# Cross-attention on one core: where the first block of x is loaded and split, and when the probability chunks are taken

## The chip, the cores and the metric

The kernel runs on one core of one Trainium2 chip. The metric is the device time of a run in microseconds; the figure given for a kernel is the median over its runs. One further execution is profiled, and every duration of a single instruction in this document comes from such a profile.

## The reference, cut to what matters

The input x (`hidden_states`) has 32 blocks of 512 rows and 640 columns, the context (`encoder_hidden_states`) 32 blocks of 77 rows and 1024 columns. For each block, text cross-attention with 20 heads of 32 is computed:

```python
q = _heads(hidden_states @ to_q_w)
h_txt = _sdpa(q, _heads(ehs_txt @ to_k_w), _heads(ehs_txt @ to_v_w))
# _sdpa: softmax(q k^T / sqrt(32)) v, for each head
out = _merge(h_txt) + ...
out = out @ to_out_w + to_out_b
out = (out + residual) / RESCALE          # RESCALE = 1, residual = x
```

The context has 77 rows in each block, so the parts for objects, others and images are empty and are left out of the kernel.

## The kernel before, in words

All products are made in a split form: an operand is written as a high part and the remainder (`split`: ScalarE copies to a rounded type, VectorE or GpSimd subtracts), and each product is three matmuls (high x high, high x low, low x high: `PAIRS`).

The program has two stages. The first makes keys and values of all 32 x 77 = 2464 context rows, in five groups of at most 512 rows (`GROUPS_KV`, the last has 416). For a group, `context` loads and transposes context rows and splits them into eight tiles `ct`; `keys` multiplies them with `wk_s` (five column tiles j, each a chain of 24 matmuls into PSUM `pk`), splits the result (`ks`) and stores it to DRAM (`k_dram`); `context_values` makes the values of 128 rows and half of the columns (a "half": 24 matmuls into `pv`), splits them into `vs`, and after the second half stores them to `v_dram`. In the last group there are four row tiles (three of 128, one of 32), so eight halves. Stage one is placed by a scheduler, which follows the program's order as far as operands allow.

The second stage is written out by hand (`manual_schedule`): each engine does its instructions in the program's order, and so does the queue of SyncE (SP), which issues all DMAs. Its unit is a slot n = 5 b + j: block b of 512 rows, and one of five column tiles j with 4 heads each; there are 160 slots. `slot(n)` (L557) issues, in this order mixed over the engines:

- scores of slot n in four row tiles t (`scores`, L368), each with a maximum on VectorE (`nm`) and four exponentials on ScalarE (`exps`, L386);
- queries of slot n + 1 (`queries`, L333, 15 matmuls in parts of 6 and 9), then `split_q` (L344 to L350), which fills `qt` with three forms of q;
- for slot n - 1: reciprocal of the sums, `normalize` on GpSimd (L401), `transpose_p` on VectorE (L408) into `z`, and four stores of z to a DRAM tile `pd`; this is a "chunk" of probabilities, which comes back in another layout by `load_p` into `raw`;
- for an older slot, its chunk is "taken": `cast_p`, `rest_p`, `last_p` split `raw` into `pp` on ScalarE, VectorE and GpSimd (L432 to L446), `values` (L460) multiplies it with the block's values `vb`, and `split_a` splits the result into `at`;
- for the block before or the one before that, two pieces of the output projection (`piece`, L490, 12 matmuls each), addition of bias and residual, and the store;
- refills of keys and values of the next block, loads of the next x (`load_x`), its transposes in place (`transpose_x`) and splits (`split_x`, five column tiles `xt`).

Which slot takes which chunk is in `takes` and `seconds`. The distance is `LAG` = 3 slots. But the tiles for `raw`, `pp`, `at` and the output weights `wo_s` (pool `late`) lie where the weights `wv_s` and the tiles `ct` of stage one lay, and their PSUM banks where `pv` was; they exist only after the last halves of values are made. The first `LATE` slots therefore run without takes, and some chunks are taken late:

```python
    LATE = 4
    LAG = 3
    takes = {n + LAG: n for n in range(N) if n + LAG > LATE}
    seconds = {LATE + n: n for n in range(LATE + 1 - LAG)}
    takes[LATE + 1], seconds[LATE + 1] = 1, 2
```

So in slot 4 chunk 0 is taken as a `second`, at the very end of the slot; in slot 5 chunk 1 in the slot's usual place and chunk 2 as a `second`; from slot 6 on there is one take a slot, of chunk n - 3. The projection begins in slot 7 (`PIECES`: block 0 is projected in slots 7 to 11).

Between the two stages stands a run-up: x of block 0 is loaded after the last keys are stored, two halves of values are made while it is under way, x is transposed (L273) and split (L280, L281), four more halves follow, then the first queries; the last two halves stand in slots 1 and 3 (`beside`). The tiles of x (`xs`, one buffer; `xt`, seven) lie in the pool `main`, which takes the room of the pool `kvt` (raw weights, raw context, `wk_s`, `ks`).

Of the kernel before, what the change touches and what calls it, by code (L numbers as in the profile page):

```python
# [8 lines left out]
F32 = mybir.dt.float32  # L9
FPR = mybir.dt.float32r  # L10
# [40 lines left out]
def kernel(  # L51
# [52 lines left out]
        nc.scalar.copy(hi, src)  # L104
        nc.vector.tensor_tensor(lo, src, hi.bitcast(F32), ALU.subtract)

    def split_weights(pool, dst, w, k, permuted=True, scale=None):


        raw = pool.tile([P, C], F32, tag="wraw", name="wraw", bufs=3)  # L110
        if permuted:
            rows = w.rearrange("(q c i) n -> c q i n", q=4, i=Q)[k]
            for q in range(4):
                nc.sync.dma_start(raw[q * Q : (q + 1) * Q, :], rows[q])  # L114
        else:
            nc.sync.dma_start(raw, w[k * P : (k + 1) * P, :])
        if scale is not None:
            scaled = pool.tile([P, C], F32, tag="wscaled", name="wscaled", bufs=1)
# [6 lines left out]
    wq_s = const.tile([P, NC_, 2, C], FPR, name="wq_s")  # L125


    kvp = tc.alloc_tile_pool(name="kvp", bufs=1, side="right")
    kvt = tc.alloc_tile_pool(name="kvt", bufs=2, side="right")
    psk = tc.alloc_tile_pool(name="psk", bufs=8, space=PSUM)  # L130
    wv_s = kvp.tile([P, NK, 2, C], FPR, name="wv_s")
    wk_s = kvt.tile([P, NK, 2, C], FPR, name="wk_s", bufs=1)
# [3 lines left out]
    def context(g0, gn):  # L136
        na = gn // Q
        src = ehs_flat[g0 : g0 + gn, :].rearrange("(a j) (q u) -> q j a u", j=Q, q=4)
        cts.clear()
        loads = {}  # L140
        k0 = 0
        for kn in (1, 1, 2, 4) if g0 == 0 else (4, 4):
            loads[k0] = kn
            k0 += kn
        for k in range(NK):
            if g0 == 0:
                split_weights(kvt, wk_s[:, k], wk, k)
            if k in loads:
                kn, k0 = loads[k], k
                cs = kvt.tile([P, G // Q, 4 * Q], F32, tag="cs", name="cs", bufs=3)  # L150
                for q in range(4):
                    nc.sync.dma_start(
                        cs[q * Q : (q + 1) * Q, :na, : kn * Q], src[q, :, :, k * Q : (k + kn) * Q]
                    )
            raw = kvt.tile([P, G], F32, tag="craw", name="craw")
            nc.vector.transpose(
                raw[:, :gn].rearrange("p (a j) -> p a j", j=Q),
                cs[:, :na, (k - k0) * Q : (k - k0 + 1) * Q],
            )
            ct = kvp.tile([P, 2, G], FPR, tag="ct", name="ct", bufs=9)  # L160
            split(ct[:, 0, :gn], ct[:, 1, :gn], raw[:, :gn])
            cts.append(ct)
# [20 lines left out]
                        ks[w * 64 : w * 64 + 64, int(half != w), :gn].bitcast(F32),  # L183
                    )

    values_of = {}

    def context_values(g0, gn, t0, h, pool):

# [20 lines left out]
        if h == 1:  # L210
# [2 lines left out]
                vs[:tn].rearrange("p h d a -> p (h d a)").bitcast(F32),  # L213
            )


    zero = kvt.tile([P, G], FPR, name="zero", tag="craw")
    nc.vector.memset(zero.bitcast(F32), 0.0)
# [6 lines left out]
        nc.tensor.matmul(warm, zero[:, :P], zero, start=True, stop=True)  # L225
    for g0, gn in GROUPS_KV:
        context(g0, gn)
        if g0 == 0:
            for k in range(NK):
                for j in range(NC_):  # L230
                    keys(g0, gn, j, k)
            for k in range(NK):
                split_weights(kvt, wv_s[:, k], wv, k)
            nc.sync.dma_start(bias, bo.unsqueeze(0).to_broadcast([P, C]))
        else:
            for j in range(NC_):
                for k in range(NK):
                    keys(g0, gn, j, k)
        if g0 == GROUPS_KV[1][0]:
            for k in range(NC_):  # L240
                split_weights(kvt, wq_s[:, k], wq, k, scale=SCALE)
        if g0 == GROUPS_KV[2][0]:
            for k in range(NC_):
                ws = kvt.tile([P, 2, C], FPR, tag="ws", name="ws", bufs=1)
                split_weights(kvt, ws, wo, k, permuted=False)
# [11 lines left out]
    psv = tc.alloc_tile_pool(name="psv", bufs=3, space=PSUM, side="right", reuse_waits="tile")  # L257
    late = []

    xts, raws, pps, ats, xss, pds, sms, pqs, pas, xrs, pos = ({} for _ in range(11))  # L260

    def load_x(b, quarters=range(4)):

        if b not in xss:
            xss[b] = main.tile([P, S // Q, C // 4], F32, tag="xs", name="xs")
        xs = xss[b]
        src = x[b].rearrange("(a j) (q u) -> q j a u", j=Q, q=4)
        for q in quarters:
            nc.sync.dma_start(xs[q * Q : (q + 1) * Q, :, :], src[q])

    def transpose_x(b, i):
        part = xss[b][:, 4 * i : 4 * i + 4, :].rearrange("p a u -> p (a u)")
        nc.vector.transpose(part, part)  # L273

    def split_x(b, c, engine=nc.gpsimd):

        xt = main.tile([P, 2, S], FPR, tag="xt", name="xt", bufs=7)
        src = xss[b].rearrange("p (a t) u -> p t a u", t=NQ)[:, :, :, c * Q : (c + 1) * Q]
        parts = [xt[:, i, :].rearrange("p (t a j) -> p t a j", t=NQ, j=Q) for i in range(2)]
        nc.scalar.copy(parts[0], src)  # L280
        engine.tensor_tensor(parts[1], src, parts[0].bitcast(F32), ALU.subtract)  # L281
        xts[b, c] = xt

    kbs, vbs, pnb = [], [], []
    for g, (j0, nj) in enumerate(GROUPS):
# [140 lines left out]
    def cast_p(n):  # L428

        raw = raws[n]  # L430
        pp = late[0].tile([P, 5, S], FPR, tag="pp", name="pp", bufs=1)
        nc.scalar.copy(pp[:, 0:2, :], raw[:, 0:2, :])  # L432
        pps[n] = pp
# [33 lines left out]

    def split_a(n):
        if n >= N - NC_ + 1:
            at = main.tile([P, 2, S], FPR, tag="xt", name="at", bufs=7)  # L470
        else:
            at = late[0].tile([P, 2, S], FPR, tag="at", name="at", bufs=8)
        split(at[:, 0, :], at[:, 1, :], pas.pop(n))
        ats[n] = at
# [46 lines left out]
            if h == 1:  # L521
                nc.sync.dma_start(out[b, t * P : (t + 1) * P, :], xr)

    LATE = 4
    LAG = 3

    takes = {n + LAG: n for n in range(N) if n + LAG > LATE}
    seconds = {LATE + n: n for n in range(LATE + 1 - LAG)}
    takes[LATE + 1], seconds[LATE + 1] = 1, 2

# [9 lines left out]
    def take(m):  # L540
        values(m)
        split_a(m)
# [11 lines left out]
        elif j == 3:  # L554
            load_values(b, 1, segments)

    def slot(n, beside=None):  # L557
        b, j = divmod(n, NC_)
        ahead, more = n + 1 < N, b + 1 < B
        back, first = PIECES[j]  # L560
        bo_, has_out = b - back, b >= back
        xsplits = SPLIT_X.get(j, ((), ())) if more else ((), ())
        turns = TRANSPOSE_X.get(j, ((), (), ())) if more else ((), (), ())
        taken, second = takes.get(n), seconds.get(n)

        refill(b, j, 0)
        if taken is not None:
# [204 lines left out]
```

## Time and profile before

| | before |
|---|---|
| time, median of 3 runs | 2010.02 us (2009.55 to 2010.04) |
| profiled execution, its own time | 1996.0 us |
| its span, first to last instruction | 1994.2 us |
| mean granted TensorE clock | 0.991 |
| busy: PE, weight loads, VectorE, ScalarE, GpSimd | 98%, 88%, 68%, 80%, 49% |
| DMA | 423.54 MB, 212 GB/s over the span |

In the profile's lines PE is TensorE's matmuls, PEld its weight loads, DVE VectorE, ACT ScalarE, POOL GpSimd, SP SyncE's queue. Times are microseconds from the span's start. `L386` is line 386 of the kernel. "out<-in" names the tiles written and read, "x40" is a count, and "[6.43 <-ACT pp L432]" says that the engine stood idle for 6.43 us before the instruction, and that the last thing it waited for was ScalarE writing `pp` in line 432. A line of windows gives the stretch, its length, the busy time of each engine with the number of instructions, the clock that TensorE was granted (1.00 is full), the share in which the 16 DMA engines were busy, and GB/s.

### The profile page before, as it was taken

The page shows a single profiled execution, that of the slowest core. Times are in us where ns is not written, and L with a number is a line of the kernel's source. Part 1 is how long each engine was busy: PE and PEld are TensorE (multiplying, and loading weights), DVE is VectorE, ACT ScalarE, POOL GpSimd, SP SyncE. Part 2 cuts the span into 40 slices and gives each one's busy share as a digit, 9 for nine tenths or more (in the row PEclk, how much of TensorE's full clock was granted, in tenths as well). Part 3 has the DMA queues.
Part 4 walks back from the last instruction along what each step waited for, and adds up shares of the span by engine and source line. Part 5 has one row for each costly group of instructions (what it writes and reads, how often), then busy time and mean ns, then how long its engine had stood idle before and what let it go on. Part 6 is the DMA issues. An engine that isn't in the chain of part 4 may idle for free.

```text
span 1994.2 us, 38184 instructions
## 1 busy us (share of the span) xinstructions
PE 1950.5 (98%) x11012; PEld 1760.0 (88%) x11012; DVE 1352.5 (68%) x2159; ACT 1598.2 (80%) x6377; POOL 982.8 (49%) x617
## 2 busy tenths in 40 slices
PE   8999997899999999999999999999999999999998
PEld 7889986788899999899899898999989898988997
DVE  4443225777777777777777777777777777777774
ACT  3321128899999999999899999999999899998993
POOL 0000023555555555655556655566655566555554
PEclk9999998999999999999999999999999999999999
DMA  7994366889988889898988899998888888888975
GB/s 172 225 261 107 106 148 146 232 213 232 226 225 226 229 221 231 216 229 212 232 225 224 220 225 230 229 233 222 219 223 223 223 223 225 224 218 230 228 198 164
DMA packets 555997, 423.54 MB, mean 212 GB/s; under 512 B 170192, under 2 KB 459502, under 8 KB 555790
## 3 DMA queue, kind: packets, MB, share of 16 engines
q1 hardware_dynamic: 555789, 421.10, 83.9%
q8 instruction: 91, 1.49, 0.3%
q14 instruction: 117, 0.95, 0.2%
HBM read 245.61 MB, written 175.32 MB: 211 GB/s over the span
## 4 chain that ended last, share of the span: by engine, by line
PE 78%; DMA 9%; SPq 4%; POOL 3%; ACT 2%; issue 2%; DVE 2%; DVEq 0%; ACTq 0%; POOLq 0%
PE po L490 24%; PE pq L333 24%; PE pa L460 13%; PE sc L368 9%; PE pv L197 4%; PE pk L168 4%; DMA raw<-pd 3%; POOL pn L401 2%; DMA pd<-z 2%; SPq L114 1%; DMA xs<-in_x_dram 1%; POOL pp L446 1%; ACT pn L386 1%; DMA k_dram<-ks 1%; DMA cs<-in_ctx_dram 1%
## 5 line engine op out<-in xcount | busy, mean ns | idle before, releaser
L386 ACT ACTIVATE pn<-sc,nm 128x77 f32<-128x77 f32 x2560 | 802.0, 330 | 44.6 <-DVE nm L376 33.8
L401 POOL TENSOR_TENSOR pn<-pn,rs 128x1232 f32<-128x1232 f32 x160 | 364.4, 2277 | 670.3 <-DVE rs L396 643.9
L490 PE MATMUL po<-wo_s,at 128*128 128x320 f32 x3840 | 626.9, 312 | 2.2 <-DVE xr L518 2.2
L333 PE MATMUL pq<-xt,wq_s 128*128 128x512 f32 x2400 | 622.4, 400 | 0.0
L490 PEld LDWEIGHTS po<-wo_s,at 128*128 128x128 f32 x3840 | 566.3, 189 | 2.7 <-DVE xr L518 2.5
L386 ACT ACTIVATION_READ_ACCUMULATOR pn<-sc,nm 128x1 f32 x2560 | 533.1, 208 | 0.0
L333 PEld LDWEIGHTS pq<-xt,wq_s 128*128 128x128 f32 x2400 | 429.6, 190 | 77.4 <-POOL xt L281 0.2
L376 DVE TENSOR_REDUCE nm<-sc 128x4 f32<-128x308 f32 x640 | 294.6, 460 | 298.2 <-PE sc L368 291.0
L460 PE MATMUL pa<-pp,vb 128*128 128x512 f32 x1280 | 334.9, 402 | 18.4 <-ACT pp L432 9.8
L460 PEld LDWEIGHTS pa<-pp,vb 128*128 128x128 f32 x1280 | 243.5, 198 | 62.8 <-POOL pp L446 14.3
L408 DVE STREAM_TRANSPOSE z<-pn 128x1280 f32<-128x1280 f32 x160 | 241.5, 1509 | 36.2 <-POOL pn L401 31.6
L439 DVE TENSOR_TENSOR pp<-raw,pp 128x1024 fp32r<-128x1024 f32 x160 | 196.1, 1226 | 82.4 <-ACT pp L432 72.2
L368 PEld LDWEIGHTS sc<-kc,qt 128*128 128x128 f32 x1280 | 212.8, 189 | 27.2 <-ACT qt L348 4.2
L446 POOL TENSOR_TENSOR pp<-raw,pp 64x512 fp32r<-64x512 f32 x160 | 209.4, 1309 | 37.0 <-ACT pp L438 19.8
L368 PE MATMUL sc<-kc,qt 128*128 128x154 f32 x1280 | 222.9, 255 | 4.5 <-DVE qt L350 3.9
L350 DVE TENSOR_TENSOR qt<-pq,qt 64x512 fp32r<-64x512 f32 x320 | 214.3, 670 | 7.5 <-ACT qt L344 3.1
L281 POOL TENSOR_TENSOR xt<-xs,xt 128x512 fp32r<-128x512 f32 x157 | 200.0, 1296 | 19.4 <-ACT xt L280 12.5
L483 POOL TENSOR_TENSOR xr<-xr,bias 128x640 f32<-128x640 f32 x128 | 201.3, 1573 | 9.7
L348 ACT CAST qt<-qt 64x512 fp32r<-64x512 f32 x320 | 198.8, 621 | 8.9
L368 PE MATMUL sc<-kb,qt 128*128 128x308 f32 x640 | 196.1, 306 | 1.2 <-ACT qt L344 1.2
L432 ACT CAST pp<-raw 128x1024 fp32r<-128x1024 f32 x160 | 170.1, 1063 | 29.7 <-DMA raw<-pd 28.9
L104 ACT CAST at<-pa 128x512 fp32r<-128x512 f32 x160 | 94.9, 593 | 82.2 <-PE pa L460 81.1
(41 smaller groups left out, 1530.8 us busy)
## 6 DMA issues: line engine op xcount, KB each, us to landing
pd<-z SPq DMA_DIRECT2D x640, 160.0 KB, 3.6
raw<-pd SPq DMA_DIRECT2D x160, 512.0 KB, 4.3
xs<-in_x_dram SPq DMA_DIRECT2D x128, 320.0 KB, 7.0
xr<-in_x_dram SPq DMA_DIRECT2D x128, 320.0 KB, 3.8
out_dram<-xr SPq DMA_DIRECT2D x128, 320.0 KB, 3.2
raw<-pd SPq DMA_DIRECT2D x160, 128.0 KB, 4.4
v_dram<-vs SPq DMA_DIRECT2D x19, 640.0 KB, 4.0
k_dram<-ks SPq DMA_DIRECT2D x80, 128.0 KB, 2.4
```

What stands on the lines that cost most here:

```text
L281: engine.tensor_tensor(parts[1], src, parts[0].bitcast(F32), ALU.subtract)
L333: nc.tensor.matmul(pqs[n], wq_s[:, k, a, j * P : (j + 1) * P], xts[b, k][:, c, :], start=(k == 0 and m == 0), stop=(k == NC_ - 1 and m == 2),)
L350: nc.vector.tensor_tensor(qt[r, 1 + w, :], pq[r], qt[r, 0, :].bitcast(F32), ALU.subtract)
L368: nc.tensor.matmul(sc[:, cols], qt[:, m, t * P : (t + 1) * P], keys_, start=(m == 0), stop=(m == 2),)
L376: nc.vector.tensor_reduce(nm, sc[:, :KCOLS].rearrange("p (h k) -> p h k", k=NKEY), AX.X, ALU.max, negate=True)
L386: nc.scalar.activation(pnb[n % 2][:, at, :NKEY], sc[:, i * NKEY : (i + 1) * NKEY], AF.Exp, bias=nm[:, i : i + 1], accum_out=sms[n][:, at : ...
L401: nc.gpsimd.tensor_tensor(pf, pf, rs.unsqueeze(2).to_broadcast([P, NQ * HPC, NKEY]), ALU.mult)
L408: nc.vector.transpose(z.rearrange("p b t j -> p t b j"), pn.rearrange("p (t h) k -> p t (h k)", t=NQ).rearrange("p t (b i) -> p t b i", i=Q),)
L446: nc.gpsimd.tensor_tensor(pp[64:, 4, :], raw[:64, 2, :], pp[:64, 4, :].bitcast(F32), ALU.subtract)
L460: nc.tensor.matmul(pas[n], vb[:, t, :, a], pp[:, c, :], start=(m == 0), stop=(m == len(PASSES) - 1),)
L483: nc.gpsimd.tensor_tensor(xrs[b, t], xrs[b, t], bias, ALU.add)
L490: nc.tensor.matmul(pos[b, t, h][:, :HALF], ats[b * NC_ + j][:, a, t * P : (t + 1) * P], wos[0][:, j, c, h * HALF : (h + 1) * HALF], start= ...
```

## The change

1. Raw weights and raw context get pools of their own (`kvw`, `kvc`), which are released when the last group's context is in `ct`. A new pool `xpool` with `xs` and `xt` takes that room, so that x of block 0 is loaded, transposed and split inside stage one, beside the last group's keys; x of block 1 is loaded right after.
2. In the run-up the queries of block 0 come first, then four halves of values with the transposes of block 1's x and two of its splits between them. The other four halves stand in slots 0 and 1, two in each.
3. `LATE` is 2, and all chunks are taken three slots after their own (`takes` alone; `seconds` is gone). The output weights' loads, which stand in slots `LATE` to `LATE + 2`, come two slots earlier with it.

Subtractions of block 0's x are all on GpSimd (before, three of five on VectorE). The number of matmuls does not change.

```diff
-    def split_weights(pool, dst, w, k, permuted=True, scale=None):
-        raw = pool.tile([P, C], F32, tag="wraw", name="wraw", bufs=3)
+    def split_weights(dst, w, k, permuted=True, scale=None):
+        raw = kvw.tile([P, C], F32, tag="wraw", name="wraw", bufs=3)
...
+    kvw = tc.alloc_tile_pool(name="kvw", bufs=1)
     kvp = tc.alloc_tile_pool(name="kvp", bufs=1, side="right")
     kvt = tc.alloc_tile_pool(name="kvt", bufs=2, side="right")
+    kvc = tc.alloc_tile_pool(name="kvc", bufs=3, side="right")
...
-                cs = kvt.tile([P, G // Q, 4 * Q], F32, tag="cs", name="cs", bufs=3)
+                cs = kvc.tile([P, G // Q, 4 * Q], F32, tag="cs", name="cs", bufs=3)
...
     for g0, gn in GROUPS_KV:
         context(g0, gn)
+        if g0 == GROUPS_KV[-1][0]:
+            kvw.release()
+            kvc.release()
+            xpool.append(
+                ctx.enter_context(tc.tile_pool(name="xpool", bufs=1, reuse_waits="tile"))
+            )
+            load_x(0)
+            for i in range(NQ):
+                transpose_x(0, i)
+            for c in range(NC_):
+                split_x(0, c)
+            load_x(1)
...
-    LATE = 4
+    LATE = 2
     LAG = 3
 
-    takes = {n + LAG: n for n in range(N) if n + LAG > LATE}
-    seconds = {LATE + n: n for n in range(LATE + 1 - LAG)}
-    takes[LATE + 1], seconds[LATE + 1] = 1, 2
+    takes = {n + LAG: n for n in range(N)}
...
-    def slot(n, beside=None):
+    def slot(n, beside=()):
...
-        xsplits = SPLIT_X.get(j, ((), ())) if more else ((), ())
-        turns = TRANSPOSE_X.get(j, ((), (), ())) if more else ((), (), ())
-        taken, second = takes.get(n), seconds.get(n)
+        xsplits = SPLIT_X.get(j, ((), ())) if more and n > LATE else ((), ())
+        turns = TRANSPOSE_X.get(j, ((), (), ())) if more and b else ((), (), ())
+        taken = takes.get(n)
...
-        if beside:
-            beside()
+        if len(beside) > 0:
+            context_values(*beside[0], psv)
         s = scores(n, 3)
...
         exps(n, 3, *s)
+        if len(beside) > 1:
+            context_values(*beside[1], psv)
         if has_out:
             piece(bo_, first + 1)
...
-        if second is not None:
-            cast_p(second)
-            rest_p(second)
-            last_p(second)
-            take(second)
-            if second + 2 in pds and second + 2 not in takes.values():
-                load_p(second + 2)
...
     with tc.manual_schedule(engines=ENGINES):
         g0, gn = GROUPS_KV[-1]
-        load_x(0)
         load_keys(0, 0)
-        for h in range(2):
-            context_values(g0, gn, 0, h, psv)
-        for i in range(NQ):
-            transpose_x(0, i)
-        for c in range(NC_):
-            split_x(0, c, nc.gpsimd if c % 2 else nc.vector)
-        load_x(1)
-        for t0 in (P, 2 * P):
-            for h in range(2):
-                context_values(g0, gn, t0, h, psv)
+        halves = [(g0, gn, t0, h) for t0 in range(0, gn, P) for h in range(2)]
         queries(0, 0, NC_)
         split_q(0)
+        for half in halves[:2]:
+            context_values(*half, psv)
+        for i in range(NQ):
+            transpose_x(1, i)
+        for c in range(2):
+            split_x(1, c)
+        for half in halves[2:4]:
+            context_values(*half, psv)
         for n in range(LATE):
-            slot(n, (lambda: context_values(g0, gn, 3 * P, n // 2, psv)) if n % 2 else None)
+            slot(n, halves[4 + 2 * n : 6 + 2 * n])
...
         load_p(0)
-        load_p(1)
```

`load_x`, `transpose_x` and `split_x` are the same functions as before, moved up and with `xpool` in place of `main`.

More of the change, by code (lines that the diff above doesn't have):

```diff
@@ L117, in split_weights @@
         if scale is not None:
-            scaled = pool.tile([P, C], F32, tag="wscaled", name="wscaled", bufs=1)
+            scaled = kvw.tile([P, C], F32, tag="wscaled", name="wscaled", bufs=1)
             nc.scalar.mul(scaled, raw, scale)
@@ L146, in context @@
             if g0 == 0:
-                split_weights(kvt, wk_s[:, k], wk, k)
+                split_weights(wk_s[:, k], wk, k)
             if k in loads:
                 kn, k0 = loads[k], k
-                cs = kvt.tile([P, G // Q, 4 * Q], F32, tag="cs", name="cs", bufs=3)
+                cs = kvc.tile([P, G // Q, 4 * Q], F32, tag="cs", name="cs", bufs=3)
                 for q in range(4):
@@ L184, in keys @@
                     )
-    values_of = {}
+    values_of, xts, xss, xpool = {}, {}, {}, []
     def context_values(g0, gn, t0, h, pool):
@@ L214, in context_values, with load_x, transpose_x, split_x @@
             )
+    def load_x(b, quarters=range(4)):
+        if b not in xss:
+            xss[b] = xpool[0].tile([P, S // Q, C // 4], F32, tag="xs", name="xs")
+        xs = xss[b]
+        src = x[b].rearrange("(a j) (q u) -> q j a u", j=Q, q=4)
+        for q in quarters:
+            nc.sync.dma_start(xs[q * Q : (q + 1) * Q, :, :], src[q])
+    def transpose_x(b, i):
+        part = xss[b][:, 4 * i : 4 * i + 4, :].rearrange("p a u -> p (a u)")
+        nc.vector.transpose(part, part)
+    def split_x(b, c, high=nc.scalar.copy, low=nc.gpsimd):
+        xt = xpool[0].tile([P, 2, S], FPR, tag="xt", name="xt", bufs=7)
+        src = xss[b].rearrange("p (a t) u -> p t a u", t=NQ)[:, :, :, c * Q : (c + 1) * Q]
+        parts = [xt[:, i, :].rearrange("p (t a j) -> p t a j", t=NQ, j=Q) for i in range(2)]
+        high(parts[0], src)
+        low.tensor_tensor(parts[1], src, parts[0].bitcast(F32), ALU.subtract)
+        xts[b, c] = xt
     zero = kvt.tile([P, G], FPR, name="zero", tag="craw")
@@ L232 @@
             for k in range(NK):
-                split_weights(kvt, wv_s[:, k], wv, k)
+                split_weights(wv_s[:, k], wv, k)
             nc.sync.dma_start(bias, bo.unsqueeze(0).to_broadcast([P, C]))
@@ L240 @@
             for k in range(NC_):
-                split_weights(kvt, wq_s[:, k], wq, k, scale=SCALE)
+                split_weights(wq_s[:, k], wq, k, scale=SCALE)
         if g0 == GROUPS_KV[2][0]:
             for k in range(NC_):
-                ws = kvt.tile([P, 2, C], FPR, tag="ws", name="ws", bufs=1)
-                split_weights(kvt, ws, wo, k, permuted=False)
+                ws = kvw.tile([P, 2, C], FPR, tag="ws", name="ws", bufs=1)
+                split_weights(ws, wo, k, permuted=False)
                 nc.sync.dma_start(wo_dram[:, k].bitcast(F32), ws.bitcast(F32))
@@ L258 @@
     late = []
[L260 to L282, printed above, removed]
+    raws, pps, ats, pds, sms, pqs, pas, xrs, pos = ({} for _ in range(9))
     kbs, vbs, pnb = [], [], []
@@ L469, in split_a @@
         if n >= N - NC_ + 1:
-            at = main.tile([P, 2, S], FPR, tag="xt", name="at", bufs=7)
+            at = xpool[0].tile([P, 2, S], FPR, tag="xt", name="at", bufs=7)
         else:
```

## The prediction

> **What bounds the kernel now.** First the page's busy shares and slices, then PE's waits, then windows around the one place where PE is not full, then that place's timeline on PE and ACT.
>
> ```profile
> PE 1950.5 (98%) x11012; PEld 1760.0 (88%) x11012; DVE 1352.5 (68%) x2159; ACT 1598.2 (80%) x6377; POOL 982.8 (49%) x617
> PE   8999997899999999999999999999999999999998
> PEclk9999998999999999999999999999999999999999
> ```
> PE is the bound everywhere but in the first slices and in slices 6 and 7 (about 299 to 399 us). In steady slots it has no gap: scores start at 390.27 and again at 400.60, so a slot is 10.33 us of PE work (from the starts in PE's timeline): queries 3.53, scores 4 x 0.33, values 1.87, projection 2 x 1.80.
>
> ```profile
> 265.00:283.00 18.00, 17.81 (x122) 17.54 (x120) 5.96 (x9) 3.78 (x8) 8.88 (x8) 1.00 0.72 148
> 283.00:294.00 11.00, 7.50 (x40) 6.45 (x40) 4.34 (x7) 2.68 (x7) 1.81 (x2) 1.00 0.79 155
> 294.00:334.00 40.00, 34.86 (x183) 28.15 (x182) 23.84 (x43) 35.11 (x167) 15.33 (x9) 0.96 0.50 121
> 334.00:344.00 10.00, 3.92 (x8) 2.77 (x9) 4.44 (x5) 5.25 (x20) 1.74 (x1) 0.57 1.13 248
> 344.00:360.00 16.00, 11.71 (x45) 9.09 (x44) 8.99 (x13) 11.06 (x41) 5.32 (x3) 0.82 0.94 232
> 380.00:390.00 10.00, 10.00 (x59) 9.04 (x58) 6.76 (x12) 9.87 (x40) 7.71 (x6) 1.00 0.83 224
> ```
> Columns: length, then busy time of PE, weight loads, DVE, ACT, POOL, granted clock, DMA share, GB/s. Read PE against the length: the loss lies between the last keys (end 265.2) and slot 8. Between 294 and 334 ACT is the fuller engine; between 334 and 344 PE is nearly empty and its clock falls to 0.57.
>
> ```profile
> PE pa L460 <- ACT pp L432: 9.8, 2, 6.4
> PE sc L368 <- DVE qt L350: 3.9, 6, 1.6
> PE pv L197 <- DVE vs L105: 3.0, 1, 3.0
> 339.62 0.80 PE L460 MATMUL pa<-pp,vb 128*128 128x512 f32 x1 [6.43 <-ACT pp L432]
> 355.54 0.54 PE L460 MATMUL pa<-pp,vb 128*128 128x512 f32 x1 [3.38 <-ACT pp L432]
> 318.27 0.41 PE L368 MATMUL sc<-kc,qt 128*128 128x154 f32 x1 [0.42 <-ACT pn L386]
> 318.48 2.85 PE L333 MATMUL pq<-xt,wq_s 128*128 128x512 f32 x6
> ```
> The 6.43 and 3.38 us are the first "second" takes, at the ends of slots 4 and 5: the cast of a chunk stands behind the slot's last exponentials on ACT, and PE has nothing else in its order.
>
> How much is lost: PE work from 265.2 to the start of slot 8 is 8 value halves x 3.52, queries 0 to 8 (9 x 3.53), 8 slots' scores x 1.33, 5 takes x 1.87, slot 7's projections 3.60: 83.5 us, that is 348.7. Slot 8 starts at 379.94. So 31 us is all that this change can touch; from slot 7 on, by the instruction lists, both programs issue the same instructions in the same order on all five engines, and before the last group's keys too.
>
> **The change part by part**, on the profiled execution's own time (1996.0 us, span 1994.2; the runs' median, 2010.02, is 14 us above; I carry the difference over unchanged).
>
> *x of block 0 under the last keys.* Moved: four loads, four transposes, five copies (ACT), five subtractions (now all POOL). In SP's order the loads follow the last value store of group 3, whose issue ends at 244.77. Before, the first load's issue at 268.19 led to the first transpose at 277.58, 9.4 us: x is there at about 254. Transposes 3.0 (257.1), copies 2.7 (259.8), subtractions 5 x 1.28 to 1.48 (264.5 at the latest). PE needs the first at 265.2 and the fifth at 268.0: covered, slack 3.5. Queued behind them are the last keys' casts and subtractions (0.51 + 0.59 each) and their stores; PE waits for none of those but through PSUM, where five of eight banks are used in turn. Bounds: 0 to 1.2 us (a bank held by the last keys' eviction); I take 0.
>
> *Loads behind that.* The second x load waits for POOL's last subtraction (264.5), and on SP the last key stores and the eight key loads of block 0 are queued behind it; each DMA also waits for the one eight places before it. Before, from the first x issue to the last of these key loads took 9.3 us (277.47), and they landed 5 to 6 us after issue in that stretch: at best 280, at worst 284. They are needed at 282.8 (next step). Cost 0 to 1.5, I take 0.4.
>
> *Queries first, then the value halves.* PE: 265.2 + 3.53 + 4 x 3.52 = 282.8, slot 0. The 3.0 us wait for vs goes: nothing is queued before that eviction but one 1.9 us split of q. Slots 0 and 1 now hold two halves each: 1.33 + 3.53 + 7.04 = 11.9 us of PE against ACT's 7.4 (exponentials 4.85, q 1.9, evictions 0.65). PE-bound; slot 1 ends at 306.6. Before it ended at 310.0, and two halves were still to come.
>
> *Chunks at distance 3 throughout.* No take in slot 2, one per slot from 3 on. Now ACT is the longer: casts 1.56, exponentials 4.85, q 1.9, at 0.5, waits on nm 0.55, makes 9.4 us a slot against PE's 6.73. Walked through in queue order, with the rows' durations. Slot 2: first nm 308.2 (behind the last eviction's low half), exponentials to 309.4 and 310.6, queries done 310.8, split of q 311.1 to 313.0, exponentials to 314.2; meanwhile POOL's normalisation (2.28) ends 310.7, z's transpose (1.50) 312.3, q's low half (1.4) 313.6, last nm 314.1, last exponentials 315.4. A slot with a take, counted from its cast: exponentials end at 2.8; nm 1, behind the chunk's low half and the reciprocal, at 2.9; exponentials 4.15; split of q 6.05; exponentials 7.3; at 7.8; on the side normalisation to 4.85, z 6.3, q's low half 7.7 (here PE's next slot opens), nm 3 8.2; last exponentials 9.4. Slot 3 has three copies of x besides, 10.55. So slot 3's cast starts at 315.4, slot 4's at 325.95, then 335.35, 344.75 and, slot 7, 354.15. Before, slot 7's cast started at 370.90: 16.75 us earlier. PE's slot 7 and what follows hang on the same cast in both.
>
> *What is late next: the chunks' way through DRAM.* wo's five loads (640 KB each) come two slots sooner, between these chunks. Chunk 0's load needs the last value matmul (its buffer lies in the old weights): issue 308.4, landing 4.5 to 6.4 later, needed 315.4. Chunk 1: about 325, needed 326. Chunk 2: about 334.2, needed 335.35. Chunk 3: its store waits for z, the load is behind x's second half, a wo part and four key loads: issue 339.5, and with the 6.9 us that a chunk took behind x and wo (issue 341.98) it lands at 346.5, needed 344.75: 1.8 late. With the best landing, 4.5 us (362.48), it is in time; with 8 to 10 us for chunk, x and wo, as between 331 and 344, the three together are about 8 late. Cost 0 to 8, I take 1.8: the wo pair at 358.73 landed in 4.4 to 5.1, and here the first pair meets as little.
>
> *The clock.* The row first: at 318.48 six query matmuls took 2.85 us (1.59 at full clock), after gaps of 0.50, 1.56 and 0.42. [...] The queries have 2.8 us of slack before ACT takes them, so most hides: 0 to 5 us, I take 0.5, nearer the row but hidden.
>
> *Rest.* Block 1's transposes and two copies go from slots 1 and 2 to before slot 0, where DVE and ACT idle; they delay one value eviction by 2 us, whose bank is not needed for 8 more. Nothing else is added.
>
> Sum: 16.75 - 0.4 - 1.8 - 0.5 = 14.0. Profiled time 1982.0; median 2010.0 - 14.0 = **1996.0**.
>
> **The rivals.**
> 1. *DMA becomes the bound in slots 4 to 6.* For: between 334 and 360 its share is 0.94 to 1.13, and wo's 3.2 MB now come in the same slots as five chunks out and in. Against: 294 to 334 stands at 0.50, and wo's descriptors are long. Price 8 instead of 1.8: 2002.2.
> 2. *PE behind x or the keys.* x lands 5 us later than before's 9.4, or key loads late: PE stands before queries or scores of slot 0, 3 to 6 us, partly taken back because ACT-bound slots follow: 1999 to 2002.
> 3. *ACT's loop is tighter*: waits on nm vanish (0.55 x 4) and no chunk is late: gain 18.5 to 19, 1991.2.
> 4. *Slower: the clock stays at half through slots 2 to 6.* It decides from 6.73 / 9.4 = 0.72 down: below that PE is the longer loop. At 0.5: slot 2 9.7, four slots of 13.5, slot 7 2.5 longer until the clock is back: slot 7 in effect at 372.6 against before's 369.6 (367.98 and 1.6 of its own waits). 2013. For: 0.57 between 334 and 344. Against: that followed 6.43 us without a matmul; slots 294 to 334, at 87% busy, had 0.96.
> 5. *Doesn't do what it says*: the loads stay late because SP is in order. The issue order has x of block 0 ahead of the last keys' stores, so hardly.
>
> **How the numbers follow.** The forecast (gain 11 to 17) 0.55; DMA-bound 0.15; x or keys late 0.10; tighter loop 0.11; half clock 0.03; an unnamed loss that leaves a gain under 4 us or none, 0.06. A measurement of this kernel tells about 0.2%, 4 us, from no change. Faster by more: 0.88 (all but the last two and a little of rival 1); within 0.07; slower 0.05. Range 1990 to 2003: tighter loop below, DMA-bound above; some 2 in 10 lie outside.
>
> **What would show it.** In the profile after: PE with no wait over 1 us from 265 to about 306; queries before the values' last group; slot 1 ending near 306.6; no wait of 6 us for pp; ACT near full from 308 to 355 with slots of 9.4; slot 7's cast near 354 to 356. Wrong: PE waiting for xt (POOL) or kb at 265 or 283; ACT waiting for raw by more than 3 us; clock under 0.72 between 310 and 350; any change in the steady slot of 10.33.

## The result, and the profile after

The changed kernel takes 1980.45 us (median of 4 runs, 1979.49 to 1980.79) against 2009.78 for the kernel before (4 runs, 1994.61 to 2010.04): ratio 0.9868 [0.9846, 0.9891], 29 us faster. The forecast was 1996.0, its range 1990 to 2003: the sign was right, the gain forecast (14 us) half of the one measured. The profiled execution took 1980.38 us, its span is 1978.6. One thing is needed to read the numbers below: the kernel before spreads by 7 to 15 us between the executions of one set of runs (single runs from 1994.6 to 2013.6, medians of the sets from 2005.8 to 2009.8), the changed one by 1.3 here, so that the profile shown for the kernel before, 1996.0, is one of its fast executions and the two profiles are only 15.6 us apart.

The page of the changed kernel, PE's busy share in 40 slices:

```profile
PE   9999998999999999999999999999999999999998
```

PE's dip in slices 6 and 7 is nearly filled. Windows from slot 3 to slot 7 (length, then busy time of PE, weight loads, DVE, ACT, POOL, granted clock, DMA share, GB/s):

```profile
316.00:326.00 10.00, 8.02 (x37) 6.66 (x38) 6.24 (x10) 9.50 (x40) 4.02 (x3) 0.92 1.02 259
326.00:336.00 10.00, 8.21 (x34) 6.57 (x34) 6.07 (x10) 9.76 (x40) 6.81 (x5) 0.84 0.90 244
336.00:346.00 10.00, 7.48 (x30) 5.67 (x29) 3.71 (x8) 6.25 (x28) 2.28 (x2) 0.90 1.13 245
346.00:356.00 10.00, 7.88 (x31) 6.24 (x31) 6.39 (x10) 6.53 (x28) 1.26 (x1) 0.83 1.03 227
356.00:366.00 10.00, 7.50 (x25) 6.08 (x26) 7.99 (x14) 9.08 (x41) 3.54 (x2) 0.66 0.77 195
```

Until 336 ACT fills its time (9.5 and 9.8 of 10), as forecast. Then it falls to 6.3 and 6.5 while the DMA share is 1.13 and 1.03: transfers, not ACT, set slots 5 and 6. ACT's timeline names them, at the casts of the chunks for slots 3 to 7 (the last line is slot 7's cast in the kernel before):

```profile
317.58 1.05 ACT L445 CAST pp<-raw 128x1024 fp32r<-128x1024 f32 x1
327.99 1.09 ACT L445 CAST pp<-raw 128x1024 fp32r<-128x1024 f32 x1
341.01 1.05 ACT L445 CAST pp<-raw 128x1024 fp32r<-128x1024 f32 x1 [3.16 <-DMA raw<-pd]
353.53 1.05 ACT L445 CAST pp<-raw 128x1024 fp32r<-128x1024 f32 x1 [2.90 <-DMA raw<-pd]
363.43 1.05 ACT L445 CAST pp<-raw 128x1024 fp32r<-128x1024 f32 x1
```

```profile
370.90 1.05 ACT L432 CAST pp<-raw 128x1024 fp32r<-128x1024 f32 x1
```

Slot 7's cast comes at 363.43 and not at 354.15; before it was 370.90. So the profile gives the run-up 7.5 us at that cast, and 6.3 at the start of PE's slot 8 (373.60 against 379.94), where 14 had been forecast, and yet the whole gain is twice the forecast. The rest lies where nothing was expected: in the steady slots. From the values of slot 9 to those of slot 153 PE goes from 396.60 to 1891.26 before and from 390.19 to 1873.81 after: 10.38 us and 10.30 us a slot on the mean, 11.0 us over these 144 slots. (Behind slot 153 the changed kernel's execution is 1.8 us longer.) Waits and windows of the kernel before, between 400 and 1880 us (engine, line and tile that waited, what ended it: total, times, longest):

```profile
ACT pp L432 <- DMA raw<-pd: 28.9, 25, 2.2
PEld pa L460 <- POOL pp L446: 10.5, 14, 2.0
400.00:1000.00 600.00, 597.28 (x3407) 539.50 (x3406) 449.70 (x718) 548.40 (x2251) 347.70 (x216) 1.00 0.89 224
1000.00:1900.00 900.00, 897.77 (x5122) 811.44 (x5121) 673.30 (x1077) 827.31 (x3394) 533.10 (x334) 1.00 0.89 225
```

The same of the changed kernel:

```profile
ACT pp L445 <- DMA raw<-pd: 3.2, 4, 1.5
PEld pa L473 <- POOL pp L459: 0.6, 1, 0.6
400.00:1000.00 600.00, 599.83 (x3435) 543.89 (x3434) 452.74 (x723) 552.26 (x2271) 353.97 (x221) 1.00 0.89 226
1000.00:1900.00 900.00, 900.00 (x5159) 816.75 (x5158) 676.44 (x1084) 829.55 (x3406) 533.20 (x333) 1.00 0.88 225
```

Before, chunks came late to their cast 25 times, and part of that reached PE, which lost 5.0 us to gaps and had most slots between 10.31 and 10.33 us, but 14 of the 144 longer; after, it has 0.2 us of gaps and slots of 10.29 to 10.31, with one longer. The instructions of these slots and their order are the same in both kernels.

All 25 late chunks are of one kind, those of slots 5 b + 3. SP issues x's four loads in slot 5 b + 4, two ahead of that chunk's stores and two behind them, and all four stand ahead of the chunk's load. SP's own waits between 400 and 1880 us, of the kernel before (L425 is the second part of a chunk's load, L310 a load of keys just behind it):

```profile
SPq L425 <- DMA xs<-in_x_dram: 24.6, 27, 2.1
SPq L310 <- DMA xs<-in_x_dram: 23.5, 29, 2.4
```

Of the changed kernel:

```profile
SPq L438 <- DMA xs<-in_x_dram: 17.4, 26, 1.2
SPq L323 <- DMA xs<-in_x_dram: 15.5, 29, 1.2
```

Once in a block SP holds the second part of the chunk's load until x has landed, for 24.6 us in all before and 17.4 after. (In every one of these waits the load of x stands eight places ahead in SP's queue; in both traces none of SP's 2573 DMAs is issued before the one eight places ahead of it has landed.) The load of x shows which transfer became cheaper. Before, in the page's rows of DMA issues (the last column is the median from issue to landing):

```profile
xs<-in_x_dram SPq DMA_DIRECT2D x128, 320.0 KB, 7.0
out_dram<-xr SPq DMA_DIRECT2D x128, 320.0 KB, 3.2
```

After:

```profile
xs<-in_x_dram SPq DMA_DIRECT2D x128, 320.0 KB, 6.1
out_dram<-xr SPq DMA_DIRECT2D x128, 320.0 KB, 3.0
```

Same bytes, same pieces. What differs is the address. In the built program x's landing tile `xs` starts at byte 100032 of each partition before, which is 64 past a multiple of 128, and at 44672 after, a multiple of 128. The seven buffers `xt` of split x behind it moved in the same way; every other tile of the slots kept its place modulo 512.

### The profile page after: what moved, and what is told of

Its sections match the earlier page's. It is cut to its first block, busy times and chain, and to the rows that moved or that the text cites. A ratio compares the mean times of both kernels' runs of the same rounds, so it can differ in the third digit from the quotient of the medians.

```text
span 1978.6 us, 38192 instructions
## 1 busy us (share of the span) xinstructions
PE 1946.0 (98%) x11012; PEld 1761.7 (89%) x11012; DVE 1345.8 (68%) x2156; ACT 1595.6 (81%) x6377; POOL 986.0 (50%) x620
## 3 DMA queue, kind: packets, MB, share of 16 engines
q8 instruction: 91, 1.49, 0.3%
## 4 chain that ended last, share of the span: by engine, by line
PE 90%; DMA 4%; SPq 2%; ACT 1%; DVE 1%; issue 1%; POOL 1%; DVEq 0%; ACTq 0%; POOLq 0%
PE po L503 28%; PE pq L346 28%; PE pa L473 15%; PE sc L381 10%; PE pv L200 4%; PE pk L171 4%; DMA raw<-pd 1%; SPq L114 1%; DMA k_dram<-ks 1%; SPq L155 1%; DMA v_dram<-vs 1%; DMA wraw<-in_L_xattn_to_k_w_dram 0%; POOL pn L414 0%; DMA wraw<-in_L_xattn_to_out_w_dram 0%; DMA cs<-in_ctx_dram 0%
## 5 line engine op out<-in xcount | busy, mean ns | idle before, releaser
L238 POOL TENSOR_TENSOR xt<-xs,xt 128x512 fp32r<-128x512 f32 x160 | 203.9, 1292 | 269.2 <-ACT xt L237 262.0
```

The costliest lines, as they stand in the source:

```text
L238: low.tensor_tensor(parts[1], src, parts[0].bitcast(F32), ALU.subtract)
```

## The experiments

Times are medians; each ratio is against the kernel before on the same chip in the same job (one set of runs). e1 to e4, e5 to e8, e9 to e12 and e13 with e14 are one job each. The expectations are on record as they stood before each run.

| run | what | us | ratio to before |
|---|---|---|---|
| e1 | before, unchanged | 2006.92 | 0.9997 [0.9979, 1.0014] |
| e2 | new pools, old order | 1986.45 | 0.9899 [0.9880, 0.9918] |
| e3 | new pools, early x, old takes | 1984.68 | 0.9890 [0.9869, 0.9911] |
| e4 | old pools, distance 3 throughout | 2001.79 | 0.9985 [0.9973, 0.9998] |
| e5 | before, x lands 64 bytes on | 1991.67 | 0.9927 [0.9899, 0.9955] |
| e6 | after, x lands 64 bytes on | 1994.97 | 0.9946 [0.9921, 0.9971] |
| e7 | after, `xt` 64 bytes on | 1981.25 | 0.9871 [0.9846, 0.9897] |
| e8 | after, the slots' DMA tiles on 128 | 1975.61 | 0.9842 [0.9816, 0.9869] |
| e9 | before, the slots' DMA tiles on 128 | 1988.36 | 0.9898 [0.9882, 0.9915] |
| e10 | e8 less the loads of x of block 2 | 1970.89 | 0.9810 [0.9796, 0.9825] |
| e11 | e8, wo's loads spread | 1973.69 | 0.9828 [0.9812, 0.9845] |
| e12 | e11, chunk ahead of normalisation | 1975.63 | 0.9838 [0.9824, 0.9853] |
| e13 | after, x lands 32 bytes on | 1995.34 | 0.9925 [0.9903, 0.9948] |
| e14 | e11, first stage on 128 too | 1972.39 | 0.9817 [0.9799, 0.9834] |

**Which part brings it: e1 to e4.** The change was taken apart into its pools, its early x and its takes.

e1_before_again, no edit: 

> The kernel before, unchanged, with a profile of its own. Three theories of the 15 us by which before's median gained more than its profiled execution. Phase theory (before has more than one steady course: chunks come back from DRAM later in the slot, ACT's cast waits for raw, PE waits now and then, and which course a run falls into is left over from its start): runs of this kernel spread over 1994 to 2010 on one chip, and a slow run shows steady slots over 10.33 us with waits for raw. Layout theory: all runs of this kernel alike within 1 us of each other in steady slots. Chip theory (the 2010 runs come from another chip): all runs here at 1994 to 1996.

e2_layout_only, the tiles as after, the order as before (shortened):

```diff
-    raw = kvt.tile(..., tag="wraw", ...)     # ws, wscaled likewise; cs in kvc
+    raw = kvw.tile(..., tag="wraw", ...)
-    xs, xt: main.tile(...)
+    xs, xt: xpool[0].tile(...)
```

> Pools and addresses of the kernel after (raw weights, raw context and x in pools of their own), but the order, LATE = 4 and the second takes of before. Layout theory: steady slots as after (10.30 us, waits for raw under 5 us between 400 and 1900), 1985 to 1987. Phase theory: as before, 1994 to 2010, with waits for raw near 29 us.

e3_early_x_only, the changed kernel with the old takes (shortened):

```diff
-    LATE = 2
+    LATE = 4      # and the "second" takes as before
```

> x under the last keys and queries first as after, but LATE = 4 and the second takes of before, two halves of values in slots 1 and 3. By the prediction's sum this part alone saves PE's waits before slot 0 (4.5 us idle between 280 and 294) and little more, since the takes' waits of 6.4 and 3.4 us stay: about 5 us below before in the run-up. Phase theory: the steady course is seeded by the takes, so it is that of before, 1990 to 2005. Layout theory: steady slots as after, 1981 to 1985.

e4_late2_only, the kernel before with the new distance (shortened):

```diff
-    LATE = 4      # and "second" takes
+    LATE = 2
```

> LATE = 2 and one distance for all chunks, two halves in slots 0 and 1, with x, its loads and its pools as before. By the prediction's sum the takes' part is the larger: 9 to 12 us of the run-up. Phase theory: steady course as after, 1983 to 1987. Layout theory: steady slots as before (10.32 us, waits for raw near 29 us), 1986 to 2001.

Measured: e1 repeats the kernel before. None of its ten runs lies below 2000, so the theory of the chip falls; its profiled run, at 2008.8, has still later chunks than the one shown (38.8 us of casts' waits in 26 places after 400 us) and slots of 10.43 us on the mean. e2 alone brings 20 us of the 29, with 4.6 us of such waits and not 29, so the phase theory falls too. e3 brings 1.8 more; its values of slot 8 start 4.9 us earlier than e1's, the 5 that had been expected. e4 has the new distance and brings 4.6 of the 9 to 12 expected, with an interval that all but reaches 1; its casts wait 6.8 us for chunks in the run-up and 32.1 after 400 us. So the pools decide, and no theory of the order alone can stand. But e2 was not a pure change of place: with the buffers free earlier, its first x load goes out at 247.01 and not at 270.51 (e1), and its first queries start 4.7 us sooner. The next four runs change places alone.

**Which tile: e5 to e8.**

e5_before_xs_plus64 (e6_after_xs_plus64 and e13_after_xs_plus32 have the same edit in the changed kernel, the last with 8 for 16 words):

```diff
-            xss[b] = main.tile([P, S // Q, C // 4], F32, tag="xs", name="xs")
+            wide = main.tile([P, S * C // (4 * Q) + 32], F32, tag="xs", name="xs")
+            xss[b] = wide[:, 16 : 16 + S * C // (4 * Q)].rearrange("p (a u) -> p a u", u=C // 4)
```

> The kernel before with one edit: the tile in which x lands is 128 bytes longer and used from its 64th byte, so that x lands at byte 100096 of each partition (a multiple of 128) in place of 100032 (64 past a multiple); every other tile keeps its place or moves by exactly 128 bytes, and no instruction is added, left out or moved. Theory A (the place of x's landing buffer decides the steady slots): about 1987 us (1984 to 1991) as with the whole layout of the new pools, waits of the casts for the chunks' loads after 400 us down from about 30 us to under 10, x landing in 6.1 to 6.3 us and not 7.0. Theory B (the seven buffers of split x, or the distance of the tiles from each other, decides): no change, 2002 to 2010 us, waits of about 30 us.

> The changed kernel with x's landing tile used from its 64th byte: x lands 64 bytes past a multiple of 128, as in the kernel before; the buffers of split x and all else keep their place modulo 128. Theory A: the steady slots lose what they had won, about 1999 us (1994 to 2004), x landing in about 7.0 us, casts waiting about 30 us for chunk loads after 400 us. Theory B: as the changed kernel, 1980 us within 2.

e7_after_xt_plus64, 64 bytes behind `xs`, and 64 more behind `xt`:

```diff
-            xss[b] = xpool[0].tile([P, S // Q, C // 4], F32, tag="xs", name="xs")
+            wide = xpool[0].tile([P, S * C // (4 * Q) + 16], F32, tag="xs", name="xs")
+            xss[b] = wide[:, 0 : S * C // (4 * Q)].rearrange("p (a u) -> p a u", u=C // 4)
...
+    main.tile([P, 16], F32, name="pad0")
```

> The changed kernel with 64 bytes between x's landing tile and the seven buffers of split x, so that these start 64 bytes past a multiple of 128, as in the kernel before; x's landing tile stays on its multiple, everything behind moves by 128 bytes. Theory A: as the changed kernel, 1980 us within 2, x landing in 6.1 us. Theory B (the buffers that TensorE reads its queries' weights from decide): about 1999 us (1994 to 2004).

(In `queries` the weights are `wq_s`, the 128*128 of the profile's line; `xt` is the other operand, 128x512.)

e8_after_all_128:

```diff
         kb = main.tile([P, nj, KCOLS], FPR, name=f"kb{g}")
+        if g == 0:
+            main.tile([P, 24], F32, name="padk")
...
+        if g == 0:
+            main.tile([P, 24], F32, name="padc")
...
+        if n == 0:
+            late[0].tile([P, 8], F32, name="padr")
         raw = late[0].tile([P, 3, S], F32, tag="raw", name="raw", bufs=2)
```

> The changed kernel with small unused tiles between others, so that every tile that a DMA writes or reads in the slots (keys, the transposed probabilities z, the chunks raw, the values, wo, xr) starts on a multiple of 128 bytes; before, most start 32 or 64 bytes past one. Theory A read widely (any DMA is dearer by some per cent at such a place): the remaining waits of the run-up, some 8 us in slots 3 to 6, shrink, and the time falls to 1973 to 1978. Theory A read narrowly (only x's pieces of 640 bytes pay; the long rows of the chunks and the 512-byte rows of z do not, or the steady slots have no wait left to lose): 1979 to 1981.

Measured: 64 bytes take 14.1 us off the kernel before (2005.8 to 1991.67, one job) and put 14.5 onto the changed one (1980.45 to 1994.97, two jobs; 13.7 against e7 of the same job). e5, its landing row and the casts' waits between 400 and 1880 us:

```profile
xs<-in_x_dram SPq DMA_DIRECT2D x128, 320.0 KB, 6.1
ACT pp L433 <- DMA raw<-pd: 2.2, 3, 1.3
```

e6, the same two rows:

```profile
xs<-in_x_dram SPq DMA_DIRECT2D x128, 320.0 KB, 7.1
ACT pp L446 <- DMA raw<-pd: 30.3, 24, 2.7
```

Without an instruction added or moved, e5 has the fast landing and almost no late chunk, and e6 the slow landing and the late chunks of the kernel before, all 24 again of slots 5 b + 3. The steady slots carry the whole of it: over the same 144 slots the mean is 10.41 us in e6 and 10.32 in e7, 13.2 us in all, and SP waits 45.0 us for x in e6 and 32.1 in e7. The instructions that read x's tile are no part of it: a transpose takes 833 to 835 ns, a copy 634 and a subtraction 1292 to 1299, before, after, in e5 and in e6. e6 came out at the low edge of its interval, e5 just above its own (1991.67 against at most 1991). e7 is the changed kernel within 1 us: where TensorE reads split x from decides nothing of this size (its slots are 10.32 and not 10.30 on the mean, a hint of a small price). e8 goes below the changed kernel by 4.8; one wait for a chunk is left after 400 us, of 0.3 us, and the slots are 10.27 to 10.31. It did not come where it was expected: in the run-up the casts still wait 5.0 us for chunks (6.1 in the changed kernel). Of the 4.6 us between the two profiles, the 0.01 that a slot became shorter makes 1.7. The other 2.9 lie behind slot 153 (104.79 us from its values to the end after, 101.87 in e8; a last wait for DVE there fell from 2.97 to 1.45), where two executions of the kernel before differ too (102.97, and 104.79 in e1), so they are not shown to be the tiles'. Which tile brings the rest was not taken apart.

**What the order is worth, and what limits it: e9 to e12.** With the slots' tiles on 128 in both kernels, place can no longer hide the order.

e9_before_all_128 is e8's edit in the kernel before. 

> The kernel before, order untouched, with small unused tiles so that every tile that a DMA touches in the slots starts on a multiple of 128 bytes, as in the changed kernel with the same tiles (1975.6). Then the distance to 1975.6 is what the change's order alone is worth, with no place in it. If the order is worth what the two traces show (cast of slot 7 at 363.4 in place of 370.9 to 374.5, so 7.5 to 11 us): 1983 to 1987. If the prediction's 14 us for the order was right and something else hid it: 1989 to 1990. If place still differs otherwise (the absolute position of the pools): above 1990.

e10_no_x2:

```diff
     def load_x(b, quarters=range(4)):
+        if b == 2:
+            xss[2] = xss[1]
+            return
```

> The changed kernel with all tiles on 128 bytes, less the four loads of x of block 2 (1.28 MB, issued in slot 4; block 2 is computed from what lies in the tile). If the transfers are late in slots 5 and 6 because too much is moved there (the prediction's 1.8 us term, rival 1's 8): the casts' waits for raw before slot 8, 5.0 us in e8, fall under 1, slot 7's cast comes at 357 to 359 and not at 363.5, 1969 to 1971 us. If the waits come from the order of SP's queue and not from the amount: 1974 to 1976, waits of 4 to 5 us.

e11_wo_spread:

```diff
-            for k in {LATE: (0, 1), LATE + 1: (2, 3), LATE + 2: (4,)}.get(n, ()):
+        load_wo(0, 1)                      # ahead of slot 2
...
+            load_wo(*{LATE: (2,), LATE + 1: (3,), LATE + 3: (4,)}.get(n, ()))
```

> The changed kernel with all tiles on 128 bytes and wo's five loads issued apart: two before slot 2 (where the DMA share is 0.4 to 0.6), one after each of slots 2, 3 and 5, in place of two, two and one after slots 2, 3 and 4. No byte more or less. If amount in the slots 4 and 5 is what makes chunks late: waits for raw before slot 8 fall from 5.0 to 1 to 2.5 us and the time by 2.5 to 4, 1971.5 to 1973. If not: 1975 to 1976.5; if chunk 0 is made late by the pair ahead of it, 1977.

e12_wo_spread_swap:

```diff
+        if taken is not None and n < 8:
+            last_p(taken)
         if n:
             normalize(n - 1, sums(n - 1))
-        if taken is not None:
+        if taken is not None and n >= 8:
             last_p(taken)
```

> As e11, and in slots 3 to 7 the chunk's last piece stands ahead of the normalisation in POOL's queue, which takes away the waits of about 2 us of the values' products for POOL (four of them, 8.6 us in e8). The prediction has ACT's loop as the bound of these slots and PE's gaps there as free, but for the clock: then as e11 within 1 us. If the gaps are on the path: 4 to 8 us less than e11.

Measured: e9 at 1988.36 is 12.75 above e8; by the two jobs' ratios, 0.9898 and 0.9842 of some 2007, it is 11.2. It ends up between the first two expectations. Slot 7's cast, in e9 and in e8:

```profile
373.92 1.06 ACT L438 CAST pp<-raw 128x1024 fp32r<-128x1024 f32 x1
363.47 1.05 ACT L451 CAST pp<-raw 128x1024 fp32r<-128x1024 f32 x1
```

The values of slot 8 start 9.3 us apart (389.27 and 379.96), and so do those of slot 153. The other 2.7 of the 12.0 between the two profiles lie behind it (104.56 us to the end and 101.87) and are not shown to be the order's. So its own worth is 9 to 13 us. e10 leaves the four x loads out of the crowded slots (block 2 is then computed from what lies in the tile) and gains 4.7 on e8, which ran in another job, 6.4 by the two ratios. ACT's timeline of e10, slots 5 to 7:

```profile
340.14 1.05 ACT L454 CAST pp<-raw 128x1024 fp32r<-128x1024 f32 x1 [0.66 <-DMA raw<-pd]
349.65 1.05 ACT L454 CAST pp<-raw 128x1024 fp32r<-128x1024 f32 x1
359.18 1.06 ACT L454 CAST pp<-raw 128x1024 fp32r<-128x1024 f32 x1
```

One wait of 0.66 us is left, and the casts of slots 5, 6 and 7 are 9.51 and 9.53 us apart: the 9.4 that the prediction had walked out for ACT's loop. e11 moves no byte less and gains 1.9 on e8 at the median (two jobs again), with runs from 1971.5 to 1979.0, between its two expectations; two waits, of 1.49 and 1.75, stay. e12 was made to see whether PE's gaps of 2 us in these slots cost anything. PE's waits of e11 between 265 and 385 us:

```profile
PE pa L479 <- POOL pp L465: 6.7, 4, 2.5
PE sc L385 <- DVE qt L367: 2.6, 3, 1.9
```

Of e12:

```profile
PE sc L385 <- DVE qt L367: 8.2, 8, 2.9
PE sc L385 <- ACT at L104: 3.3, 2, 2.2
```

The waits for POOL are gone and others of the same size stand in their place: PE now waits for q's split, the casts are 10.4 us apart and not 9.5 as in e11, and the granted clock is 0.83 in every 10 us from 316 to 366. So the edit moved the gaps and did not take them away. It gains nothing (1975.63 against 1973.69 in the same job); what the gaps themselves cost stays open.

**On which grid, and where else: e13 and e14.**

> The changed kernel with x's landing tile used from its 32nd byte (everything behind at the places modulo 128 that it had, as in e6). If any start off a multiple of 128 pays for one more line per 640-byte piece: as e6, 1995 us (1990 to 2004), x landing in 7.0 to 7.1 us, casts waiting 25 to 35 us for raw after 400 us. If only the half-way start pays, or 32 is already an allowed step: as the changed kernel, 1980 within 2, landing in 6.1.

e14_wo_spread_stage_128:

```diff
             values_of[t0] = kvp.tile([P, HEADS, HD, 2], FPR, tag="vs", name="vs", bufs=2)
+            if t0 == 0 and g0 == 0:
+                kvp.tile([P, 24], F32, name="padv")
```

> As e11, and the tiles of the context's stage (its landing tiles, which start 96 bytes past a multiple of 128, the keys' and values' stores, the weights) moved to multiples of 128 too, by one unused 96-byte tile. If the first stage is held by its transfers as the slots were: the last keys end earlier than 266.8 by 1 to 5 us, and the time is 1969 to 1973. If it is TensorE's work that fills it (98% and more from 20 us on) or the long rows pay nothing: as e11, 1972.5 to 1975.

Measured: 32 bytes cost what 64 do (1995.34 us, and 1994.97 in e6). e13, the landing and the casts' waits from 400 to 1880 us:

```profile
xs<-in_x_dram SPq DMA_DIRECT2D x128, 320.0 KB, 7.1
ACT pp L446 <- DMA raw<-pd: 35.8, 24, 3.3
```

The good places of these runs are 128 (the changed kernel), 256 (e5) and 384 (e9) past a multiple of 512, the bad ones 160 (e13) and 192 (e6, and the kernel before): of the five starts tried, x lands in 5.9 to 6.1 us at the three on a multiple of 128, and in 7.0 and 7.1 at the two between. x lands in pieces of 640 bytes (160 numbers of a row). Time and landing are those of the expectation's first case. One line more for each piece, the reason it gives, is not shown: the runs have the landing alone, 16% longer (7.1 against 6.1), and as long from 32 past a multiple as from 64. e14 is within the spread of e11 (1972.39 and 1973.69). Its first stage did move, landings of the context's 256 KB falling from 6.7 to 6.4 us and the first queries starting at 265.34 in place of 266.99 (e11), but the first stage's end varies by 2 us between executions of one kernel (265.2 in the profile shown before, 267.5 in e1), so its worth stays open. It is the fastest version measured that leaves nothing out: 1972.39, ratio 0.9817 [0.9799, 0.9834].

## Why the prediction was wrong

**The step that failed is the one that put the steady slots at no change.** The difference between the profiled run and the median, 14 us, was carried over unchanged, on the ground that "from slot 7 on, by the instruction lists, both programs issue the same instructions in the same order on all five engines". They do, and the slots still differ, because the new pools also moved `xs` by a half step of 128 bytes. The move of the tiles appears in no part of the sum: "Nothing else is added" priced it at 0, and it measured 14.1 (e5) and 13.7 to 14.5 (e6). The path was in the prediction's own working: chunk 3 is late there because "the load is behind x's second half", and that order returns in every block. The 14 us between the profiled run and the median were a warning: the prediction had PE without a gap in the steady slots (the changed kernel, with 0.2 us of gaps there, spreads by 1.3), and the casts' waits for chunks (28.9 us in 25 places, not shown in the prediction) pointed to what varied. The prediction's own list of refutations had the right line, "any change in the steady slot of 10.33": it is 10.31, and on the mean 10.30 in place of 10.38.

**The order: right in its mechanism, put somewhat too high.** Forecast 14.0, measured 9 to 13 with place taken out (e9 to e8). With 14 for place that makes 23 to 27 of the 29; the kernel before's median in the first set lies 1 to 4 us above those of the later jobs, which can cover the rest. In the two profiles first shown the order had seemed worth only 7.5, in part because there the last keys ended 1.8 us later after the change than before it (267.0 and 265.2); in e1 and e9 they end at 267.5 and 267.3 without the change, so this is no part of it. Its terms:

- *x under the last keys*, 0: PE's first queries follow the last keys without a gap at 266.82. Right. Rival 2 falls, and rival 5 with it.
- *Queries first, then halves*: slot 1 ends at 307.95 against 306.6. Right but for the first queries, which start 1.6 later than supposed. No wait for late key loads (0.4 forecast).
- *ACT's loop*: 10.55 for slot 3 and 9.4 for the others; 10.41 in the changed kernel's slot 3, and 9.5 where the transfers allow it (e10). Right. Rival 3, a tighter loop, falls.
- *Chunks late*, 1.8 taken out of 0 to 8: the mis-sized term. The changed kernel's casts wait 3.16 and 2.90 us, the first of them over the 3 us that the list of refutations names; taking 1.28 MB out of those slots gives 4.7 to 6.4 us back (e10). Mechanism as rival 1 has it, size between the two. Its evidence, a DMA share of 0.94 to 1.13 in those slots of the kernel before, was in view and should have moved the value to the middle.
- *The clock*, 0.5: no run shows this term. What the runs show is the clock itself: in the changed kernel it is 0.66 between 356 and 366 and 0.83 between 346 and 356, windows in which no gap of PE is longer than 2.51 us; in the kernel before it is 0.50 from 319 to 321, behind the gaps of the row at 318.48. So the row was a good guide to the clock. What it cost was not separated, since e12 keeps such gaps; in e10 it is 0.83 between 346 and 356, and the casts there are 9.51 and 9.53 us apart against 9.4 walked out without it, which leaves little room. Rival 4 falls: from 316 to 366 the clock is 0.83 on the mean, over the 0.72 from which that rival decides.

**The range** was too narrow on the low side for one reason: every case in it, the rivals too, lay in the run-up. None was a case of the steady slots, 152 of the 160.

## What to carry to other kernels

A change of pools is a change of addresses: compare the built program's addresses of the tiles that DMAs land in, before calling two loops identical; here it was x's place modulo 128 (14.1 us in e5, 14.5 in e6). Where PE fills a loop but the time spreads from run to run, look at the transfers that are just in time and at what stands ahead of them in the queue; a dearer landing there, 7.1 us and not 6.1 (e6), was enough to make them late. (Off the multiple of 128 the executions of one set spread by 7 to 15 us here, on it by 1 to 8.) And separate place from order by an edit that shifts one tile by some bytes: here 64 bytes made more difference than the whole reordering.

## What the runs showed of the hardware

- A load of x (320 KB in pieces of 640 bytes) landed in 5.9 to 6.3 us where the tile started on a multiple of 128 bytes and in 6.9 to 7.1 where it started 32 or 64 past one. Other transfers of the loop paid with it: out's 320 KB took 2.7 to 3.0 us beside the good place, 3.2 to 3.4 in the kernel before, 3.5 in e6 and e13.
- The DMA share of the steady slots hardly tells the two cases apart: 0.88 to 0.90 with late chunks (before, e1, e4, e6, e13), 0.85 to 0.89 without. The landing times and the casts' waits do.
